# A store moved to POOL's DMA queue, and two steps of a DMA transpose shifted by a sub-step, in a macaron S4D block

## The chip, the cores and the metric

The kernel runs on one core of a Trainium2 chip. The time is that of the device, in microseconds (us), for one execution of the whole program. A core has five engines, each with its own in-order instruction stream: TensorE (PE; its weight loads are listed as PEld), VectorE (DVE), ScalarE (ACT), GpSimd (POOL) and SyncE (SP). SP only starts DMA transfers here; ACT and POOL start some as well. An instruction that waits holds up all that stands behind it in its stream.

## The reference

The input x has 8 sequences of 2048 tokens with 256 features. The block is

```python
x = x + 0.5 * ffn(layernorm(x))          # 256 -> 1024 -> relu -> 256
n = layernorm(x)
y = irfft(rfft(n) * rfft(K))[:length]    # causal convolution along the tokens, K from the S4D parameters
x = x + layernorm_affine(n + y + n * D)
x = x + 0.5 * ffn(layernorm(x))          # the same weights
```

with `K[h, l] = 2 Re sum_n Ct[h, n] exp(dtA[h, n] l)`: for each of the 256 features 64 complex exponentials.

## The kernel before

**Three stages.** Sublayer "a" is the first feed-forward part together with the normalization that follows it (0 to about 800 us). The convolution comes next (800 to 1000 us), and sublayer "b", the second feed-forward part, last. In "a" and "b" the tokens go through in 64 groups of 2 x 128. For each group PE makes 8 hidden chunks of 128 units: `up` (L854) needs 6 matmuls of 128x128 by 128x256, `down` (L864) another 6, since each factor is split into a high and a low part. ACT evicts the high part of a hidden chunk (`hx`, L926), DVE the low part (L116 with `hx`), and `down` follows three chunks later. Around each group there is other work: a bias addition on POOL (L777), statistics on DVE (L693, L697), small reciprocal and `q_u`, `nb_u` operations, normalizations on ACT (L730), transposes on PE (L794), a cast on ACT (L803), the closing addition `post_a` on DVE (L992). From group 44 on the transpose is made by DMA: `xp` is stored (L819) and read back turned (L823).

**The background.** While "a" runs, `matrices()` builds the tables of the convolution. It is a generator: `sublayer` draws steps from it between the hidden chunks. Its last part makes the matrix P in 32 blocks (bt 0 to 31) of 128 x 1024 numbers, and for each block both P itself (`o_dram`, used for the outputs) and its transpose (`pt_dram`, used for the states) must come to DRAM. A block passes four generators:

- `make(bt)`: six POOL operations (L600 to L610) write the block to one of four places in the big tile u (`p_of`, reused by block bt + 4).
- `spread(bt)`: ACT splits the block's 32-bit numbers into two planes of 16 bits (L620, two copies), SP stores the planes (`pv`, L623) and then the block itself (`o`, L625).
- `turn(bt)`: SP reads the planes back with a DMA transpose (L631).
- `transpose(bt)`: the join. DVE and ACT put the turned planes together in the block's place (L646, one copy each), and SP stores that (`pt`, L650).

The loop runs in cycles of six sub-steps. In cycle c the generators `transpose(c-3)`, `turn(c-2)`, `spread(c-1)` and `make(c)` each take one step a sub-step. `PX` is the number of sub-steps that `turn` lets pass first, `PY` the number that the join lets pass, `DI` the same for the copies. Beside it `lags()` runs, which adds POOL operations (L536 to L542) and small POOL DMAs (L570, four in a row) in the first 13 cycles or so.

**What sets the order.** Each engine's order is settled when the program is built. A scheduler places each operation by its own estimate of when its inputs are ready; operations marked `keep_in_program_order` stay in the order of the source among themselves. The turns, ACT's copies, the joins and L777 are so marked. The POOL operations of `make` aren't, so the scheduler may mix those of several blocks. A change in one place can thus reorder all the engines.

Of the kernel before, what the change touches and what calls it, by code (L numbers as in the profile page):

```python
# [43 lines left out]
def macaron_s4d_kernel(  # L44
# [17 lines left out]
    nc = tc.nc  # L62
# [152 lines left out]
    o_dram = [dram.tile([P, BCH * P], F32, name=f"o_{i}") for i in range(NBT)]  # L215
# [42 lines left out]
    def matrices():  # L258
# [207 lines left out]
        for i in range(H // P):  # L466
            nc.gpsimd.dma_start(
                out=kpad[i * P : (i + 1) * P, P + 1 :], in_=zeros[:, 0 : P - 1]
# [6 lines left out]
        with nc.allow_non_contiguous_dma(reason="256 numbers"):  # L475
            nc.gpsimd.dma_start(
                out=kpad.rearrange("(g c) k -> c g k", c=2)[:, :, P], in_=k0
# [100 lines left out]
        def p_of(bt):  # L578

            r, i = (room[2], 28 + bt % 4 * 8) if bt < first else (room[3], (16, 24, 48, 56)[bt % 4])  # L580
            return r[:, i * P : (i + 8) * P]

        def tmp_of(bt):
            tm = room[2][:, 60 * P : 64 * P] if bt < first else room[3][:, 0 : 4 * P]
            return tm.rearrange("p (g a b) -> p g a b", g=PB, a=NA)

        def make(bt):

            E = G_
            pp = p_of(bt).rearrange("p (r g k) -> p r g k", r=2, g=PB)  # L590
            tm = tmp_of(bt)
            gs = slice(bt * PB, (bt + 1) * PB)
            br, bi = (
                pb[:, ri, gs, ::-1].unsqueeze(2).to_broadcast([P, PB, NA, NB]) for ri in range(2)
            )
            ar, ai = (
                pa[:, ri, gs, ::-1].unsqueeze(3).to_broadcast([P, PB, NA, NB]) for ri in range(2)
            )
            pr, pi = (pp[:, ri].rearrange("p g (a b) -> p g a b", b=NB) for ri in range(2))
            E.tensor_mul(pr, br, ar)  # L600
            yield
            E.tensor_mul(tm, bi, ai)
            yield
            E.tensor_sub(pr, pr, tm)
            yield
            E.tensor_mul(pi, br, ai)
            yield
            E.tensor_mul(tm, bi, ar)
            yield
            E.tensor_add(pi, pi, tm)  # L610
            yield

        def spread(bt):

            pl = planes[:, bt % 2]
            pu = p_of(bt).bitcast(U16).rearrange("p (m w) -> p w m", w=2)
            for _ in range(DI):
                yield
            for w in range(2):
                tc.keep_in_program_order(A_.copy(pl[:, w], pu[:, w]))  # L620
                yield
            via = pv_dram[bt % 2]
            nc.sync.dma_start(out=via, in_=pl.rearrange("p w m -> p (w m)"))  # L623
            yield
            nc.sync.dma_start(out=o_dram[bt], in_=p_of(bt))  # L625
            yield

        def turn(bt):
            for _ in range(PX):
                yield  # L630
            ins = nc.sync.dma_start(  # L631
                out=planes[:, bt % 2].rearrange("p w (k n) -> p (w k) n", n=P),
                in_=pv_dram[bt % 2], transpose=True,
            )
            if PINT:
                tc.keep_in_program_order(ins)
            yield

        def transpose(bt):
            pl, ptb = planes[:, bt % 2], p_of(bt)  # L640
            for _ in range(PY):
                yield
# [9 lines left out]

        planes = wpool.tile([P, 2, 2, BCH * P], U16, name="planes", tag="wE")
        P_REINT = (V.tensor_copy, A_.copy)
        PY = 0
        BACK = 3
        DI = 2
        PX = 2
        PA = 9.1
        PB_ = 10.3  # L660
        PPIN = 1
# [2 lines left out]
        for bt in range(NBT + BACK):  # L664
            parts = []
            if 0 <= bt - BACK < NBT:
                parts.append(transpose(bt - BACK))
            if 0 <= bt - 2 < NBT:
                parts.append(turn(bt - 2))
            if 0 <= bt - 1 < NBT:  # L670
                parts.append(spread(bt - 1))
            if bt < NBT:
                parts.append(make(bt))
            for n in range(6):
                for p in parts:
                    next(p, None)
                next(beside, None)
                yield (PA if bt < first + BACK else PB_) / 6
            if bt == first + BACK - 1:
                yield "half"  # L680
# [554 lines left out]
    def begin():  # L1235
        for _ in range(sizes[1] // PB):
            next(head)

    sublayer(
        w1t, w2t, pre_a, post_a, 18, "a", load_weights(), chain(matrices(), early()),  # L1240
        {"half": NG // 2, "tables": NG * 3 // 4},
        {NG * SLOTS - 6: lambda: next(head), NG * SLOTS - 1: begin},
# [127 lines left out]
```

## Time and profile before

| what | value |
|---|---|
| median of 8 runs | 1762.92 us (1759.86 to 1769.06) |
| the profiled execution's own time | 1765.73 us |
| its span, first to last instruction | 1763.7 us |
| mean granted clock of TensorE | 0.994 |
| PE busy | 1726.4 us, 98% |
| DVE, ACT, POOL busy | 1369.7, 985.3, 589.4 us |
| blocks of P are made from / to | 194 us (first L600) / 598.6 us (last store pt) |
| `o`, `pv`, `pt` stores | 32 each, 512 KB, 3.6 us from issue to landing (median) |
| turn of planes | 32, 6.2 us from issue to landing (median) |
| L620 / L646 on ACT / L646 on DVE, median | 1.05 / 1.36 / 0.84 us |
| six operations of `make`, one each | 1.06 us (multiplications), 1.30 us (addition, subtraction) |

The 40 slices of the page show PE at 9 tenths or more in nearly all, and POOL full between about 180 and 330 us:

```profile
PE   8999999989999999999999799999999999999998
POOL 1117989875775115110000122222222222222220
```

In such a row each digit stands for 44 us. Timeline lines begin with start and length in us; a bracket at the end gives the idle time of the engine just before, and what ended it. "SPq" and "ACTq" are instructions that start a DMA; their length is that of the issue, not of the transfer.

### The profile page before, as it was taken

What the parts mean: (1) busy time and instruction counts of PE and PEld (TensorE: products, weight loads), DVE (VectorE), ACT (ScalarE), POOL (GpSimd) and SP (SyncE); (2) the same over time, 40 slices, a digit from 0 to 9 for tenths busy, and PEclk for the clock granted to TensorE, in tenths of its full rate; (3) what the DMA queues carried; (4) which work ended last, traced back from release to release, by engine and by line L of the source; (5) the groups of instructions that cost most, each with busy time, mean ns of one, the idle gap of its engine ahead of it and who ended that gap; (6) DMA issues with size and microseconds to landing.
All of it is one profiled execution on the core that took longest, in us unless ns stands there. A gap on an engine that the chain in (4) does not pass through costs nothing.

```text
span 1763.7 us, 40994 instructions
## 1 busy us (share of the span) xinstructions
PE 1726.4 (98%) x15367; PEld 1697.8 (96%) x15367; DVE 1369.7 (78%) x4405; ACT 985.3 (56%) x2178; POOL 589.4 (33%) x550
## 2 busy tenths in 40 slices
PE   8999999989999999999999799999999999999998
PEld 7999999989999999999999799999999999999998
DVE  6998877767776667766999788888888888888884
ACT  4555477667777755544555445555554555555553
POOL 1117989875775115110000122222222222222220
PEclk9999999999999999999999999999999999999999
DMA  5111177669878533346998813333333333333331
GB/s 189 49 37 52 49 216 225 212 190 269 233 230 240 162 103 96 93 113 193 263 268 261 267 52 93 97 91 86 95 91 97 91 96 94 87 94 94 92 94 50
DMA packets 293277, 242.68 MB, mean 138 GB/s; under 512 B 164564, under 2 KB 237012, under 8 KB 292566
## 3 DMA queue, kind: packets, MB, share of 16 engines
q1 hardware_dynamic: 265648, 206.36, 41.5%
q10 hardware_dynamic: 26502, 32.52, 5.6%
q8 instruction: 120, 1.97, 0.5%
q0 software_dynamic: 928, 1.19, 0.3%
q14 instruction: 79, 0.65, 0.1%
HBM read 91.89 MB, written 109.84 MB: 114 GB/s over the span
## 4 chain that ended last, share of the span: by engine, by line
PE 71%; DMA 5%; DVE 1%; SPq 1%; ACT 1%; POOL 0%; issue 0%; ACTq 0%; DVEq 0%; POOLq 0%
PE po_b L864 20%; PE ph_b L854 20%; PE ph_a L854 10%; PE po_a L864 10%; PE pv L1097 3%; PE py L1163 3%; PE py L1172 3%; DMA planes<-pv 2%; DMA pt<-pt 1%; DMA pt_b<-xp 0%; SPq L631 0%; DMA wb<-w_dram 0%; DMA ot<-o 0%; PE pe L1215 0%; DVE u L646 0%
## 5 line engine op out<-in xcount | busy, mean ns | idle before, releaser
L864 PE MATMUL po_a<-wa,hx_a 128*128 128x256 f32 x3072 | 456.1, 285 | 11.5 <-DVE hx_a L116 11.3
L854 PE MATMUL ph_a<-xh_a,wa 128*128 128x256 f32 x2048 | 456.2, 287 | 1.8 <-DVE wa L195 1.1
L864 PE MATMUL po_b<-wb,hx_b 128*128 128x256 f32 x3072 | 442.0, 283 | 2.7 <-DVE hx_b L116 2.6
L854 PE MATMUL ph_b<-xh_b,wb 128*128 128x256 f32 x2048 | 443.6, 284 | 0.7 <-ACT xh_b L803 0.7
L864 PEld LDWEIGHTS po_a<-wa,hx_a 128*128 128x128 f32 x3072 | 406.6, 192 | 14.3 <-DVE hx_a L116 13.8
L864 PEld LDWEIGHTS po_b<-wb,hx_b 128*128 128x128 f32 x3072 | 401.0, 192 | 3.4 <-DVE hx_b L116 3.3
L854 PEld LDWEIGHTS ph_a<-xh_a,wa 128*128 128x128 f32 x2048 | 355.9, 193 | 4.6 <-ACT wa L194 1.5
L854 PEld LDWEIGHTS ph_b<-xh_b,wb 128*128 128x128 f32 x2048 | 353.8, 193 | 1.1 <-ACT xh_b L803 1.1
L926 ACT ACTIVATE hx_b<-ph_b 128x256 fp32r<-128x256 f32 x512 | 191.4, 381 | 237.8 <-PE ph_b L854 226.0
L926 ACT ACTIVATE hx_a<-ph_a 128x256 fp32r<-128x256 f32 x512 | 194.7, 387 | 231.3 <-PE ph_a L854 220.8
L116 DVE SCALAR_TENSOR_TENSOR hx_a<-ph_a,hx_a 128x256 fp32r<-128x256 f32 x512 | 209.1, 414 | 123.3 <-ACT hx_a L926 121.7
L854 PE MATMUL ph_a<-xl_a,wa 128*128 128x256 f32 x1024 | 290.3, 285 | 0.0
L854 PE MATMUL ph_b<-xl_b,wb 128*128 128x256 f32 x1024 | 285.7, 284 | 0.0
L1305 POOL TENSOR_TENSOR xb<-xb,lnb_sb 128x512 f32<-128x512 f32 x64 | 83.1, 1300 | 510.3 <-DMA xb<-x_dram 341.7
L116 DVE SCALAR_TENSOR_TENSOR hx_b<-ph_b,hx_b 128x256 fp32r<-128x256 f32 x512 | 210.8, 414 | 52.6 <-ACT hx_b L926 45.4
L854 PEld LDWEIGHTS ph_a<-xl_a,wa 128*128 128x128 f32 x1024 | 197.5, 193 | 0.8 <-DVE xl_a L805 0.4
L854 PEld LDWEIGHTS ph_b<-xl_b,wb 128*128 128x128 f32 x1024 | 198.0, 193 | 0.1
L777 POOL TENSOR_TENSOR xa<-xa,hb 128x512 f32<-128x512 f32 x64 | 88.9, 1389 | 278.8 <-ACT xn L730 242.3
L730 ACT ACTIVATE xn<-xb,nb_fb,t_fb 128x255 f32<-128x255 f32 x127 | 69.5, 594 | 77.5 <-DVE nb_fb L116 77.5
L777 POOL TENSOR_TENSOR xb<-xb,hb 128x512 f32<-128x512 f32 x64 | 95.1, 1486 | 52.0 <-ACT xn L730 22.7
L815 DVE COPY pl_b<-xn 128x512 uint16<-128x512 uint16 x62 | 43.6, 703 | 72.9 <-ACT xn L730 72.9
L730 ACT ACTIVATE u<-xa,nb_u,t_u 128x256 f32<-128x256 f32 x104 | 90.2, 867 | 0.0
(263 smaller groups left out, 2510.4 us busy)
## 6 DMA issues: line engine op xcount, KB each, us to landing
o<-u SPq DMA_DIRECT2D x32, 512.0 KB, 3.6
pv<-planes SPq DMA_DIRECT2D x32, 512.0 KB, 3.6
pt<-u SPq DMA_DIRECT2D x32, 512.0 KB, 3.6
tz<-kpad SPq DMA_DIRECT2D x64, 256.0 KB, 4.7
xb<-x_dram SPq DMA_DIRECT2D x64, 256.0 KB, 2.7
out_dram<-xb SPq DMA_DIRECT2D x64, 256.0 KB, 2.9
x_dram<-xa ACTq DMA_DIRECT2D x62, 256.0 KB, 2.0
xp<-pl_b SPq DMA_DIRECT2D x62, 256.0 KB, 2.0
```

The source lines that it names most:

```text
L116: return V.scalar_tensor_tensor(out=o, in0=a, scalar=s, in1=b, op0=op0, op1=op1)
L730: ins = A_.activation(dst, src, AF.Identity, bias=nb[:, i : i + 1], scale=rs[:, i : i + 1])
L777: return G_.tensor_add(xt, xt, hb2.unsqueeze(1).to_broadcast([P, NTB, H]))
L815: copy(pl[:, w], xu[:, :, :, :, w])
L854: nc.tensor.matmul(ph, wt[wp][:, dc, fs], xp[:, dc, :], start=(n == 0), stop=(n == 3 * NDC - 1))
L864: nc.tensor.matmul(po[:, i, :], hp[:, tsl], wt[wp][:, fc, :], start=(fc == 0 and i == 0 and n == 0), stop=(fc == NFC - 1 and n == 2), skip ...
L926: last[A_] = A_.activation(hh, ph, AF.Relu)
L1097: ins = nc.tensor.matmul(pv[ri][c * N : (c + 1) * N, l, j0 * B : j1 * B], pts[c][:, l, ri * N : (ri + 1) * N], some(j0, j1)[:, :, BCH * bt ...
L1163: nc.tensor.matmul(py[c][:, l, :], ucs[c][:, l, :], tzs[c][:, l, :], start=(l == 0), stop=False, skip_group_check=True,)
L1172: nc.tensor.matmul(py[c][:, l, :], xs[cs, ri, p0 + l, :], ots[ri][cs, l, :], start=False, stop=(l == PB - 1 and ri == 1), skip_group_check ...
L1305: G_.tensor_add(xt, xt, lnb_sb.unsqueeze(1).to_broadcast([P, NTB, H]))
```

## The change

The store of the block leaves `spread` and SP's queue. It is issued in `make` by POOL (`nc.gpsimd.dma_start`), behind the block's sixth operation and before the step ends, so it waits for that operation alone. `spread` has one sub-step less. The turn lets one sub-step pass instead of two, the join lets one pass instead of none. What is computed stays the same.

```diff
@@ make(bt)
             E.tensor_add(pi, pi, tm)
+            nc.gpsimd.dma_start(out=o_dram[bt], in_=p_of(bt))
             yield
@@ spread(bt)
             via = pv_dram[bt % 2]
             nc.sync.dma_start(out=via, in_=pl.rearrange("p w m -> p (w m)"))
-            yield
-            nc.sync.dma_start(out=o_dram[bt], in_=p_of(bt))
             yield
@@ matrices()
-        PY = 0
+        PY = 1
         BACK = 3
         DI = 2
-        PX = 2
+        PX = 1
```

## The prediction

> **What bounds the kernel now.** I read, in this order, the page's busy shares, the table of busy time by stretch, the waits of each engine, the chain of waits, and single stretches of the timeline. TensorE (PE) is busy 98% of 1763.7 us, so a gain can only be where it stands still or runs slowly. The table by stretch (columns: stretch, length, then busy us and count of PE, PEld, DVE, ACT, POOL, then granted clock, DMA share, GB/s) says where:
>
> ```profile
> 300.00:340.00 40.00, 39.41 (x332) 39.20 (x331) 27.43 (x74) 24.46 (x49) 33.58 (x34) 1.00 0.61 183
> 340.00:380.00 40.00, 36.81 (x292) 36.41 (x293) 31.43 (x73) 26.75 (x54) 29.90 (x29) 0.96 0.66 211
> 380.00:420.00 40.00, 35.37 (x287) 34.26 (x286) 24.93 (x72) 29.46 (x53) 29.87 (x25) 1.00 0.98 264
> ...
> 460.00:500.00 40.00, 40.00 (x338) 40.00 (x337) 28.61 (x81) 29.40 (x58) 28.04 (x24) 1.00 0.80 221
> ...
> 540.00:580.00 40.00, 37.54 (x306) 37.34 (x304) 23.93 (x77) 29.91 (x59) 17.64 (x15) 0.97 0.76 225
> 580.00:620.00 40.00, 40.00 (x330) 39.99 (x330) 27.30 (x90) 27.93 (x59) 5.45 (x5) 0.98 0.59 161
> ```
>
> Full rate is 338 matmuls in 40 us (460 to 500). Against it, (338 − count)/338 x 40 gives the us lost: 0.7, 5.4, 6.0, 0, 3.8 and 0.9 in these rows, and 0.6 and 0.7 in 220 to 260 (333) and 420 to 460 (332): 18.1 us in all while the blocks of P are made. This is the ceiling: 1765.7 − 18.1 = 1747.6. Who holds PE is in the waits between 200 and 580 us (engine, waiting line, what ended the wait: us, times, longest):
>
> ```profile
> PE po_a L864 <- DVE hx_a L116: 11.3, 8, 3.1
> SPq L625 <- POOL u L610: 90.5, 17, 37.4
> ACT u L646 <- DMA planes<-pv: 21.0, 9, 4.9
> ACT planes L620 <- POOL u L610: 3.8, 4, 1.2
> DVE u L646 <- DMA planes<-pv: 14.6, 7, 4.2
> POOL u L600 <- DMA pt<-u: 16.8, 6, 5.6
> ```
>
> PE waits only for the hidden halves hx, which ACT and DVE evict. These are held when they stand at the join (L646) of planes whose turn has not landed. Block 12 on the timeline:
>
> ```profile
> 375.39 1.05 ACT L620 COPY planes<-u 128x1024 uint16<-128x1024 uint16 x1 [0.82 <-POOL u L610]
> ...
> 377.41 0.34 SPq L623 DMA_DIRECT2D pv<-planes  x1
> ...
> 380.82 4.25 SPq L631 DMA_TRANSPOSE planes<-pv  x1
> ...
> 387.96 1.36 ACT L646 COPY u<-planes 128x1024 uint16<-128x1024 uint16 x1 [3.08 <-DMA planes<-pv]
> ```
>
> The first copy starts the moment POOL ends the block; 12.6 us later the join can start, and ACT stood idle for 3.08 of them. Such joins make the losses of 300–340, 380–420 and 420–460: **A = 7.4 us**. The 5.4 us of 340–380 (**B**) are another thing: two tiny DVE operations, 160 ns elsewhere, that read two SBUF operands while POOL runs without a pause:
>
> ```profile
> 348.46 3.08 DVE L116 SCALAR_TENSOR_TENSOR q_u<-mv_j,t_u 128x4 f32<-128x4 f32 x1
> ...
> 352.79 1.98 DVE L116 SCALAR_TENSOR_TENSOR nb_u<-mv_j,t_u 128x4 f32<-128x4 f32 x1
> ```
>
> The 3.8 + 0.9 us after 540 (**C = 4.7**) are in the chain of waits: a turn of planes holds SP's queue, and the store xp of token group 45, ready at 564.9 (its second copy ends), goes out at 567.01.
>
> ```profile
> 562.80 4.11 SPq L631
> 567.01 3.11 DMA xp<-pl_a
> ```
>
> **The change part by part.** *Stores of P leave SP.* 32 issues of 0.33 us and 90.5 us of waiting go from SP's queue. But most of that wait lay before SP had other work: the planes' store follows the second copy within 0.1 us in 24 of 32 blocks, and in the critical blocks whose landing is recorded (10, 11, 13, 14) the turn follows the landing of that store within 1.1 us. So on the path this part earns nothing in A. In C it helps: in the built order of the changed program turn 29 stands ahead of the join's store pt and no turn stands between that and xp of group 45; xp can go at 564.9, 2.1 us sooner, and the slow clock after the gap falls too. I take 4 of the 4.7; bounds 0 (SP is late for another reason) and 4.7.
>
> *The turn a sub-step sooner.* From block 20 on it goes about 2.3 us earlier (block 22: issued at 478.58 behind the store pt at 478.17, its planes written by about 476). Joins there have no idle before them: cover, so 0. Without that cover it would be worth these 2.3 us a block.
>
> *The join a sub-step later.* From block 20 on it stands 1 hidden chunk (12 matmuls, 1.44 us) later. The store pt is then as much later, and so is POOL's L600 of the block four further on, which waits for its landing (16.8 us, 6 times, above). From block 20 POOL ends 10 to 20 us ahead of ACT's copies, which hides it: 0. In blocks 4 to 15 it doesn't: there POOL starts a block 0.2 to 5 us after that landing, so 1.44 us comes on top of POOL's lag.
>
> *Stores on POOL.* The trace has no 512 KB store on POOL. Nearest rows, ns shortest/median/longest:
>
> ```profile
> L570 POOL DMA_DIRECT2D kpad<-u x16: 528/530/847, 241.8 to 348.4; - x16
> L476 POOL DMA_DIRECT2D kpad<-u x1: 1114/1114/1114, 139.0 to 139.0; - x1
> ```
>
> and 550 to 609 for the two 256 KB stores of x1 (L1006). Bounds 0.53 and 1.11; I take 0.6, by L1006, which also stores 128 long rows, plus 0.1 for the wait on L610 (the gap that POOL shows between dependent operations): 0.7 x 32 = 22 us of POOL. Behind the waiting store stand the next block's L602 and the bias addition L777, for which post_a's addition (L992) and so a PSUM bank of po waits. After block 16 POOL is idle a quarter of the time and hides it. But between 256 and 334 us POOL has hardly a pause (39.16 of 40 us in 260–300), and eight stores before block 8 ends make 8 x 0.7 = 5.6 us of lag that nothing covers (bounds 8 x 0.53 = 4.2 and 8 x 1.21 = 9.7). The join now waits for the landing of the store on POOL's queue as well (2.3 to 4.5 us in the rows of L1006 and L570); it comes 10 us later or more, which hides it.
>
> *What the lag does.* The instruction order is fixed when the program is built, and it was built with that lag. In the changed order ACT's copies of blocks 5 to 11 stand 4 to 12 hidden chunks later, the joins 4 to 8. At two places a whole token group of DVE and ACT work has been pushed into the next one's: after hidden chunks 208 and 232 (counted from the first) PE has all "down" products behind it, and next in its order are transposes of a group not yet normalized. In the order of before no such place exists. Price after 208: from its eviction on, two small DVE operations 0.3, two normalizations 1.1, one of u 0.87, two copies of planes 2.1, the cast xh 0.6: 5.0 us, in which PE has 10 matmuls, 1.2: idle 3.8. DVE has 7.1 us of work in the four chunks before it (four hx 1.65, an addition 0.68, six bn_stats 2.5, six bn_aggr 1.0, eight small ones 1.3) against 5.8: 1.3 more. And the clock: in 340–380 5.4 us were lost for 3.19 idle, in 540–580 3.8 for 2.46, so 1.3 to 2.2 more, say 1.7. Sum 6.8. After 232 the join of block 11 stands in DVE's chain, 5 chunks = 7.2 us after its copies; copies to join took 10.9 us for block 11 before (356.71 to 367.57). Less DVE's surplus of 1.3 it waits 2.5; then join 0.84, three small 0.5, normalizations 2.0, cast 0.6: 6.4, minus 1.2 of PE work: 5.2, plus 1.3 and 1.7: 8.2. Joins of blocks 5, 8 and 14 stand 3 to 6 chunks behind their copies; waits of 3.1 and 4.9 left gaps of 1.0 and 2.7 in PE before, so a wait less some 2: 1.8 + 1.0 + 1.2 = 4.0. POOL's first blocks (ACT's L620 starts 0.03 us behind L610 in 3, 4, 5): 1. Together 20.0, in place of A + B + 0.6 = 13.4: **+6.6**. Bounds: −13.4 (nothing of it happens) and +17 (lag by the 1.11 row adds 4.1, a hold like B comes once more at 5.4, and the two places cost half as much again, 7.5).
>
> **Sum:** +6.6 − 4 = +2.6 on the profiled execution's 1765.7 (span 1763.7 plus 2.0 around it): 1768.3. That execution lies 2.8 above the median of the 8 runs, 1762.9, which would give 1765.5. I take 1767.
>
> The Trainium skill, SBUF — State Buffer, section "SBUF: two separate sides", speaks against a store on POOL: its descriptors are written through the port pair that DVE's fast copies lock, and it names 620 ns alone, 3100 beside a copy. Here 16 issues of L570 took at most 847 ns, so the trace does not show it; by the page's figures, an estimate, eight stores would lag by 20 us more and the time would be near 1787. TensorE: Matmul & The Clock Gate, "What's actually happening", lets the clock halve after an idle window of about 3.4 us; here 2.46 us were enough at 575 and 2.72 at 395 were not.
>
> **Rivals.** *Faster: the joins stop waiting.* PE on the chip takes 1.44 us or more a chunk; if POOL keeps up, the pushed-together groups fill up in time, and A and C go: 1765.7 − 12.1 = 1753.6, or 1750.8 on the median. For it: POOL has 15 us idle in 220–340. Against: most of it is L600 waiting for pt, which comes later now. *No change:* what the two places cost equals what A, B and C give back, and SP's freedom is hidden, as blocks 8 to 14, whose turn is bound by the store pv and not by SP, suggest; also the case that the turn isn't sooner at all. Its time is the median, 1763. *Slower by the port:* each store starts POOL anew and a q_u or nb_u is held as at 348; it decides if three more such holds fall where ACT waits: 3 x 5.4 = 16, so 1783. For it: the holds at 243.71 (3.60) and 348.46 both follow POOL's DMA issues of L570. Against: the other two bursts of L570 held nothing over 1.3.
>
> **How the numbers follow.** Chances: forecast 0.48, faster 0.22, no change 0.22, port 0.08. A measurement of this kernel tells 0.2%, 3.5 us, from no change. Of the forecast's 0.48, 0.10 fall within that and 0.01 below; of the no-change case 0.16 within and 0.03 to each side; of the faster case 0.02 within. So faster 0.01 + 0.03 + 0.20 = 0.24, within 0.10 + 0.16 + 0.02 = 0.28, slower 0.37 + 0.03 + 0.08 = 0.48. The range must hold 8 in 10: low 1756, which leaves out the lower 0.12 of the faster case, high 1779, which holds the lag by the 1.11 row and one more hold (1767 + 9.5) and leaves out the port case's 0.08. The forecast alone: 1762 to 1776.
>
> **What would show it.** Right: POOL's stores near 0.6 us; two PE gaps of 3 to 6 us between 325 and 400, each after four pushed-up "down" products, clock below 1 behind them; no gap near 575; joins without idle from block 17. Wrong: no PE gap over 3 us before 420 (faster), DVE's two-operand operations over 2 us at several stores (port), or POOL issues over 1 us (lag).

## The result, and the profile after

| | before | after |
|---|---|---|
| median | 1764.63 us (38 runs, 1759.86 to 1770.51) | 1772.58 us (13 runs, 1769.29 to 1778.76) |
| profiled execution, its span | 1765.73, 1763.7 us | 1771.62, 1769.9 us |
| granted clock of TensorE | 0.994 | 0.992 |

The ratio is 1.0045, 95% interval [1.0034, 1.0055]: slower by some 8 us. 1767 was forecast, with 1756 to 1779 as range. The sign and the stretch were right. The size was not: +2.6 was worked out for the profiled execution, and it rose by 5.9.

In the profile after, the store is L611, and lines from 626 on stand one lower than before (join L645, `up` L853, `down` L863). The table by stretch of the changed kernel (columns as before: length, busy us and count of PE, PEld, DVE, ACT, POOL, clock, DMA share, GB/s):

```profile
300.00:340.00 40.00, 38.48 (x320) 37.79 (x318) 26.92 (x69) 23.46 (x46) 37.44 (x39) 1.00 0.58 183
340.00:380.00 40.00, 37.23 (x290) 36.45 (x291) 24.45 (x66) 25.71 (x49) 27.73 (x28) 0.96 0.74 205
380.00:420.00 40.00, 32.35 (x238) 30.86 (x236) 27.55 (x59) 27.78 (x47) 33.64 (x32) 0.87 0.73 229
420.00:460.00 40.00, 38.70 (x312) 38.70 (x313) 25.94 (x76) 33.99 (x61) 22.96 (x22) 0.96 0.89 273
...
540.00:580.00 40.00, 40.00 (x334) 39.84 (x334) 30.34 (x84) 32.61 (x64) 27.01 (x24) 1.00 0.69 229
580.00:620.00 40.00, 39.60 (x323) 38.79 (x322) 28.58 (x92) 28.98 (x60) 4.59 (x4) 1.00 0.60 185
```

Against 338 matmuls, 26.4 us are lost between 220 and 620 us (18.1 before). The loss at 380 to 420 doubled, from 6.0 to 11.8; that of 540 to 580 went from 3.8 to 0.5. The waits between 200 and 580 us (engine, waiting line, what ended the wait: us, times, longest):

```profile
POOL u L600 <- DMA pt<-u: 34.6, 11, 9.0
ACT u L645 <- DMA planes<-pv: 11.9, 8, 4.4
DVE u L645 <- DMA planes<-pv: 8.1, 9, 2.1
POOL o L611 <- POOL u L610: 6.2, 21, 0.3
PE pt_a L793 <- ACT xn L729: 5.4, 2, 5.2
PE po_a L863 <- DVE hx_a L116: 5.3, 5, 2.4
```

The joins wait less for their planes than before (20.0 instead of 35.6), but PE now waits once for 5.2 us at a transpose, whose input ACT normalizes (L729), and POOL waits twice as long for the landing of `pt`. The store itself, by the view of its line (ns shortest/median/longest), and the time to landing:

```profile
L611 POOL DMA_DIRECT2D o<-u x32: 554/594/858, 220.4 to 571.7; - x32
...
DMA to landing us min/median/max: 3.0/4.0/6.9
```

0.59 us, and 21 of 32 times 0.3 us of waiting for L610 before it: 0.9 us in these blocks, 0.8 on the mean. The two largest gaps on the timeline of the changed kernel (start, length; in brackets the idle time before and what ended it):

```profile
333.75 2.26 DVE L116 SCALAR_TENSOR_TENSOR q_u<-q_u,s_u 128x4 f32<-128x4 f32 x2
...
341.14 0.74 PE L853 MATMUL ph_a<-xh_a,wa 128*128 128x256 f32 x4 [2.44 <-ACT xh_a L802]
...
379.19 2.99 DVE L116 SCALAR_TENSOR_TENSOR q_u<-mv_j,t_u 128x4 f32<-128x4 f32 x2
...
383.48 1.35 ACT L645 COPY u<-planes 128x1024 uint16<-128x1024 uint16 x1 [4.42 <-DMA planes<-pv]
385.53 1.09 ACT L729 ACTIVATE xn<-xa,nb_u,t_u 128x255 f32<-128x255 f32 x2 [0.69 <-DVE nb_u L116]
...
386.18 1.39 PE L793 MATMUL pt_a<-ident,xn 128*128 128x128 f32 x4 [5.21 <-ACT xn L729]
```

These are the two places after hidden chunks 208 and 232. At the first, q_u on DVE took 2.26 us for two operations and the normalization had to wait. At the second two things end together: q_u is held for 2.99, and ACT stands 4.42 us at a join whose planes are late.

Behind both gaps the granted clock is low for some microseconds (third number from the end; columns as in the table by stretch):

```profile
341.00:346.00 5.00, 4.86 (x26) 4.67 (x27) 1.54 (x3) 4.02 (x9) 4.01 (x4) 0.66 0.88 284
386.00:394.00 8.00, 7.13 (x33) 6.44 (x33) 2.56 (x8) 7.16 (x14) 5.24 (x5) 0.52 0.48 180
394.00:400.00 6.00, 6.00 (x53) 6.00 (x51) 3.76 (x5) 4.20 (x7) 5.60 (x6) 1.00 0.81 188
```

From 386 to 394 a matmul takes 0.22 us, from 394 to 400 it takes 0.11.

### The profile page after: what moved, and what is told of

The parts are those of the page before. It is cut to its first block, busy times and chain, and to the rows that moved or that the text cites. A ratio compares the mean times of both kernels' runs of the same rounds, so it can differ in the third digit from the quotient of the medians.

```text
span 1769.9 us, 41000 instructions
## 1 busy us (share of the span) xinstructions
PE 1730.5 (98%) x15367; PEld 1699.2 (96%) x15367; DVE 1383.4 (78%) x4405; ACT 988.7 (56%) x2178; POOL 606.4 (34%) x582
## 4 chain that ended last, share of the span: by engine, by line
PE 78%; DMA 10%; DVE 6%; ACT 3%; issue 1%; SPq 0%; ACTq 0%; DVEq 0%
PE po_b L863 18%; PE ph_b L853 18%; PE ph_a L853 16%; PE po_a L863 16%; PE py L1171 3%; PE py L1162 3%; PE pv L1096 3%; DMA planes<-pv 2%; DMA pt_b<-xp 1%; DMA xa<-in_L_attn_x_dram 1%; DMA pv<-planes 1%; DMA pt<-pt 1%; PE pt_a L793 1%; DMA pt_a<-xp 1%; DVE hx_b L116 1%
## 5 line engine op out<-in xcount | busy, mean ns | idle before, releaser
L853 PE MATMUL ph_a<-xh_a,wa 128*128 128x256 f32 x2048 | 456.8, 288 | 4.8 <-ACT xh_a L802 3.8
L863 PE MATMUL po_a<-wa,hx_a 128*128 128x256 f32 x3072 | 453.9, 285 | 5.5 <-DVE hx_a L116 5.3
L853 PE MATMUL ph_b<-xh_b,wb 128*128 128x256 f32 x2048 | 442.6, 284 | 2.0 <-ACT xh_b L834 1.4
L863 PE MATMUL po_b<-wb,hx_b 128*128 128x256 f32 x3072 | 442.0, 283 | 0.4
L863 PEld LDWEIGHTS po_a<-wa,hx_a 128*128 128x128 f32 x3072 | 404.8, 192 | 8.1 <-DVE hx_a L116 7.3
L863 PEld LDWEIGHTS po_b<-wb,hx_b 128*128 128x128 f32 x3072 | 400.7, 192 | 1.3 <-DVE hx_b L116 1.3
L853 PEld LDWEIGHTS ph_a<-xh_a,wa 128*128 128x128 f32 x2048 | 357.2, 194 | 8.5 <-ACT xh_a L802 4.8
L853 PEld LDWEIGHTS ph_b<-xh_b,wb 128*128 128x128 f32 x2048 | 352.5, 193 | 2.8 <-ACT xh_b L834 1.8
L853 PE MATMUL ph_a<-xl_a,wa 128*128 128x256 f32 x1024 | 292.4, 287 | 0.3 <-DVE xl_a L836 0.2
L853 PE MATMUL ph_b<-xl_b,wb 128*128 128x256 f32 x1024 | 284.9, 284 | 0.0
L853 PEld LDWEIGHTS ph_a<-xl_a,wa 128*128 128x128 f32 x1024 | 199.0, 194 | 2.1 <-DVE xl_a L836 1.1
L853 PEld LDWEIGHTS ph_b<-xl_b,wb 128*128 128x128 f32 x1024 | 197.2, 193 | 0.1
L729 ACT ACTIVATE xn<-xb,nb_fb,t_fb 128x255 f32<-128x255 f32 x127 | 69.5, 594 | 78.9 <-DVE nb_fb L116 78.9
L776 POOL TENSOR_TENSOR xb<-xb,hb 128x512 f32<-128x512 f32 x64 | 94.8, 1481 | 44.2 <-ACT xn L729 21.5
L729 ACT ACTIVATE u<-xa,nb_u,t_u 128x256 f32<-128x256 f32 x104 | 89.9, 864 | 0.0
```

The source lines that it names most:

```text
L729: ins = A_.activation(dst, src, AF.Identity, bias=nb[:, i : i + 1], scale=rs[:, i : i + 1])
L776: return G_.tensor_add(xt, xt, hb2.unsqueeze(1).to_broadcast([P, NTB, H]))
L853: nc.tensor.matmul(ph, wt[wp][:, dc, fs], xp[:, dc, :], start=(n == 0), stop=(n == 3 * NDC - 1))
L863: nc.tensor.matmul(po[:, i, :], hp[:, tsl], wt[wp][:, fc, :], start=(fc == 0 and i == 0 and n == 0), stop=(fc == NFC - 1 and n == 2), skip ...
```

## The experiments

Two theories were held against each other. *Order theory*: the loss is made by the instruction order that the scheduler ("planner" in the expectations) writes down, at the pushed places. *POOL-time theory*: about 1 us more of POOL per block is what costs, whoever writes the order. Besides them stood the *port theory* (the store's descriptors hold VectorE) and the *shift theory* (the shifted sub-steps cost). Ratios are against the kernel before, with 95% intervals; a difference between two kernels is that of their ratios, times 1764 us. "Lost" is the time lost at PE in 220 to 620 us, by the count of matmuls as above.

### Stores alone, shift alone

`e1_store_only` is the change with PX and PY left at 2 and 0; `e2_shift_only` sets them to 1 and 1 and leaves the store on SP.

```diff
# e1_store_only, against before
@@ make(bt)
+            nc.gpsimd.dma_start(out=o_dram[bt], in_=p_of(bt))
@@ spread(bt)
-            yield
-            nc.sync.dma_start(out=o_dram[bt], in_=p_of(bt))
# e2_shift_only, against before
-        PY = 0
+        PY = 1
-        PX = 2
+        PX = 1
```

> The store of P on POOL alone; turn and join stay where they were before (PX = 2, PY = 0). Order theory: the building of the program saw POOL late because of the stores and put all `down` products ahead of the next group's transposes after hidden chunks 208 and 232, and this costs the time; the built order of this kernel has both places, so it expects two PE gaps of 2 to 6 us between 330 and 400 us and a time 6 to 12 us above before. Shift theory (the turn a sub-step sooner and the join a sub-step later cost the time): within 3 us of before. Port theory (descriptor writing on POOL and DVE hold each other): 6 to 12 us above, but with DVE operations over 2 us all over the blocks and no gap at the two places.

> The shift alone (PX = 1, PY = 1); the store of P stays on SP. Its built order has neither of the two places. Order theory: no gap over 3 us for that reason, a time from 6 us below before (joins of blocks 17 and later and the transposes by DMA gain) to 2 us above. Shift theory: 6 to 12 us above before. Port theory: like before, within 3 us.

Measured: e1 1783.3 us, 1.0106 [1.0091, 1.0121], 36.6 us lost. e2 1762.89, 0.9995 [0.9984, 1.0005], 15.7 lost. So the store alone costs more than twice what the change costs, and also more than the 6 to 12 us that the order and port theories gave it; the shift alone costs nothing. With the store there, the shift gives back 0.6%, some 11 us. The waits of e1 say how:

```profile
ACT u L645 <- DMA planes<-pv: 23.0, 12, 6.9
DVE u L645 <- DMA planes<-pv: 13.0, 10, 2.6
```

36.0 us of joins that wait for planes, against 20.0 with the shift. The shift theory fell here.

### Which blocks

```diff
# e3_late_blocks, against after (e8_early_blocks: the two conditions exchanged)
@@ make(bt)
-            nc.gpsimd.dma_start(out=o_dram[bt], in_=p_of(bt))
+            if bt >= first:
+                nc.gpsimd.dma_start(out=o_dram[bt], in_=p_of(bt))
@@ spread(bt)
+            if bt < first:
+                nc.sync.dma_start(out=o_dram[bt], in_=p_of(bt))
+                yield
```

> As after, but the blocks 0 to 15 store P from SP as before, and only blocks 16 to 31 from POOL. POOL issues 16 stores of 0.6 us, and the built order has neither of the two places. Order theory: the loss of after is gone, time from 5 us below before to 2 us above. Port theory or POOL-time theory (each store costs its 0.9 us somewhere): half of after's loss stays, 3 to 6 us above before.

> The counterpart of e3_late_blocks: blocks 0 to 15 store from POOL, blocks 16 to 31 from SP, the rest as in the change. The places 208 and 232 are in its built order. Order theory and the theory that POOL's lag in the early blocks is what counts: like the changed kernel, 1771 us, 1767 to 1775. A cost per store: half of the 8 us, 1767 us, and e3_late_blocks would have shown the other half, which it did not.

Measured: e3 1764.12, 1.0003 [0.9992, 1.0014], 15.7 lost, as much as e2; e8 1783.05, 1.0093 [1.0075, 1.0111], 38.3 lost. Blocks 16 to 31 may store from POOL for nothing; all of the cost comes from blocks 0 to 15. That e8 is slower than the change itself, with half its stores on POOL, no theory had expected.

### The pace

```diff
# e4_pace, against before; e5_pace_after: the same line, against after
-        PA = 9.1
+        PA = 10.3
```

> The kernel before with one number changed: the background is drawn at 10.3 instead of 9.1 per cycle in the first 19 cycles, so that fewer POOL operations fall into each hidden chunk. In its built order the join stands 13 hidden chunks behind the copies for nearly all blocks, where before had 5 to 12 in blocks 5 to 15. Order theory: the joins find their planes landed, the 7.4 us lost to them go and some of the hold by POOL too: 5 to 12 us below before, unless the later end of the blocks meets the transposes by DMA of group 44 and on (+0 to 4). POOL-time theory: the same POOL work, spread out, no more than 3 us below.

> The changed kernel with one number more: the blocks are paced at PA = 10.3 instead of 9.1, as in e4_pace. All 32 stores stay on POOL, right behind the last operation. In the built order the two places after hidden chunks 208 and 232 at which a whole group's work was pushed into the next are gone. Order theory (the loss is made by the order that the planner writes down): the cost of the store goes with the places, 1753 us, 1750 to 1758, no gap of TensorE over 2 us between 330 and 400. POOL-time theory and port theory (each store costs POOL 0.9 us, or holds VectorE, whatever the order): some 6 us or more above e4_pace, 1759 to 1764.

Measured: e4 1752.91, 0.9944 [0.9930, 0.9959], only 6.5 lost; it beats both kernels. e5 1766.12, 1.0005 [0.9992, 1.0019], 21.5 lost. In e4's waits the joins hardly appear:

```profile
ACT u L646 <- DMA planes<-pv: 1.1, 1, 1.1
```

So the part A of the loss before is cured by making the blocks at a slower pace; nothing had to leave SP for that. That was the order theory's outcome; the POOL-time theory allowed a gain of 3 us at most. e5 has no pushed place, as the order theory asked, and yet stands 11 us above e4 (e5 has the shift as well, which e4 has not); that is the POOL-time theory's outcome, and more than its figure of 6.

### One more operation in place of the store

```diff
# e6_dummy_op, against e2_shift_only
             E.tensor_add(pi, pi, tm)
+            E.tensor_mul(tm[:, 0:4], bi[:, 0:4], ar[:, 0:4])
             yield
```

> The turn a sub-step sooner and the join a sub-step later as in the change, the store on SP as before, and in place of the store on POOL one more small multiplication of POOL, 4 columns wide, behind each block's last addition; its result is not used. No DMA is on POOL's queue for o, and POOL is busy with it far less than with a store. The planner, however, writes down the same pushed places as for the changed kernel (208, 232, 248). Order theory: 1770 us, 1766 to 1776, with gaps of TensorE near 338 and 381. POOL-time and port theory (what costs is the time or the descriptors of the stores): like e2_shift_only, 1763 us, 1760 to 1765.

Measured: 1785.23, 1.0110 [1.0097, 1.0123], 39.4 lost. The added multiplication does not change what is computed. It was larger than the expectation says: the first dimension of tm is that of the groups, and the view of the line shows all 512 columns.

```profile
L611 POOL TENSOR_TENSOR u<-u x32: 1049/1061/1506, 220.1 to 582.6; 128x512 f32<-128x512 f32 x32
```

It is thus no test of order against POOL's time: it has the pushed places and also 1.06 us of POOL per block, a little more than the store's 0.9. But it has no store of `o` on POOL, and costs 20 us more than e2. So a loss of this size needs no store on POOL's queue; the port theory, by which e6 would be like e2, fell as the one cause.

### POOL's operations pinned

```diff
# e7_pinned, against after: each of the six operations of make(bt)
+            k_ = tc.keep_in_program_order
-            E.tensor_mul(pr, br, ar)
+            k_(E.tensor_mul(pr, br, ar))
...
```

> The changed kernel with the six operations of each block's product kept in the order of the program, so that the planner mixes them differently with other work; all 32 stores on POOL, PA stays 9.1. The built order has no place at which fewer than two hidden chunks are pending, beyond the two at the start. Order theory: the time of e2_shift_only, 1763 us, 1758 to 1767, no gap over 2 us at 338 and 381. POOL-time and port theory: like the changed kernel, 1770 to 1775.

Measured: 1768.35, 1.0018 [1.0006, 1.0031], 21.4 lost, with gaps of PE of 2.5, 3.3 and 3.4 us at 325, 356 and 371. It lies between the two forecasts: half of the loss goes when the order changes, half stays without any pushed place. Each of the three gaps follows a DVE operation that took far longer than elsewhere while POOL was busy (a hold, in what follows): q_u, a join's copy (0.75 us elsewhere), and q_u again.

```profile
320.30 6.45 DVE L116 SCALAR_TENSOR_TENSOR q_u<-mv_j,t_u 128x4 f32<-128x4 f32 x1
...
352.31 6.42 DVE L646 COPY u<-planes 128x1024 uint16<-128x1024 uint16 x1
...
367.31 6.83 DVE L116 SCALAR_TENSOR_TENSOR q_u<-mv_j,t_u 128x4 f32<-128x4 f32 x1
```

The second started while POOL issued a DMA of L570, the third while it issued a store.

### The order held

DVE's and ACT's order in sublayer "a" is taken as the source draws it, so that copies and joins stand at the same hidden chunks in both kernels, and only where `o` is stored from differs. It was held from hidden chunk 110 to 420; the expectation gives half of these numbers.

```diff
# e9_held_sp, against e2_shift_only; e10_held_pool, against after
# e11_held_pool_pace is e10, e12_held_sp_pace is e9, with PA = 10.3
@@ sublayer
             if t == 0:
                 ordered.close()
+            if tag == "a" and t == 110:
+                ordered.enter_context(tc.manual_schedule(engines={mybir.EngineType.Activation, mybir.EngineType.DVE}))
+            if tag == "a" and t == 420:
+                ordered.close()
```

> The shift of the change with the store on SP (as e2_shift_only), and the order of VectorE and ScalarE in sublayer a, from hidden chunk 55 to 210, held as the source draws it, so that the planner's estimate of POOL no longer decides it. The copies of blocks 0 to 31 stand 7 hidden chunks apart and the joins 12 to 15 behind their copies. This is the base of the pair with e10_held_pool: near e2_shift_only, 1764 us, 1756 to 1772 by either theory.

> The changed kernel, stores on POOL, with the order of VectorE and ScalarE held in the same way: copies and joins stand at the same hidden chunks as in e9_held_sp, and no place is pushed. Only POOL's own time and order, and where o is issued, differ. Order theory (the planner's pushes alone cost): within 3 us of e9_held_sp. POOL-time theory (0.9 us a store, 8 stores before block 8 ends, make ScalarE's copies wait for POOL, whoever writes the order): 7 us or more above e9_held_sp, with waits of the copies (L621) on POOL's last operation (L610) between 250 and 400 us.

> As e10_held_pool, with the blocks paced at 10.3 instead of 9.1, which gives POOL some 1.3 us more a block, more than a store's 0.9. POOL-time theory: the gap to e12_held_sp_pace is smaller than that of the pair before, 0 to 4 us. Order theory: no gap in either pair.

> As e9_held_sp, paced at 10.3. By either theory the best of the four, near e4_pace: 1753 us, 1748 to 1758.

| | store from SP | store from POOL |
|---|---|---|
| PA 9.1 | e9 1779.22, 1.0075 [1.0054, 1.0096], 24.4 lost | e10 1796.96, 1.0175 [1.0151, 1.0200], 41.8 lost |
| PA 10.3 | e12 1774.25, 1.0047 [1.0029, 1.0065], 19.8 lost | e11 1794.59, 1.0168 [1.0144, 1.0193], 33.7 lost |

The held order is a bad one in itself (e9 is 14 us above e2, e12 18 above e4, where both were expected to be near them). But within each pair DVE and ACT have one order (in the traces the same instructions one by one until after 1030 us), and the store on POOL costs 18 and 21 us. The order theory, by which the pairs would agree, fell. That the pace would give POOL the time back fell too. The tables of e9 and e10 by stretch, 260 to 420:

```profile
260.00:300.00 40.00, 38.62 (x322) 38.21 (x322) 30.24 (x77) 28.73 (x55) 34.01 (x35) 1.00 0.69 220
300.00:340.00 40.00, 30.50 (x251) 29.69 (x249) 24.41 (x62) 21.81 (x41) 38.00 (x38) 0.97 0.57 184
340.00:380.00 40.00, 39.96 (x316) 39.73 (x317) 30.06 (x76) 28.92 (x56) 35.62 (x33) 0.94 0.74 233
380.00:420.00 40.00, 39.40 (x329) 39.19 (x329) 30.07 (x81) 29.49 (x57) 26.96 (x23) 1.00 0.81 270
```

and e10:

```profile
260.00:300.00 40.00, 35.35 (x283) 34.80 (x281) 27.77 (x71) 24.86 (x46) 36.75 (x39) 0.96 0.72 199
300.00:340.00 40.00, 34.45 (x257) 34.25 (x258) 30.52 (x64) 24.52 (x47) 35.38 (x38) 0.87 0.63 195
340.00:380.00 40.00, 32.59 (x252) 31.95 (x252) 26.92 (x60) 22.58 (x44) 33.34 (x33) 0.91 0.54 176
380.00:420.00 40.00, 35.01 (x278) 34.81 (x277) 29.61 (x67) 26.09 (x48) 29.23 (x29) 0.91 0.74 211
```

With the store from SP most of the loss is over at 340; with it on POOL it goes on to 420, and the clock falls with each gap. How far POOL lags shows in the end of the block's last operation (L610 on the timeline, us):

| block | e2 | after | later | e9 | e10 | later |
|---|---|---|---|---|---|---|
| 4 | 262.2 | 271.4 | 9.2 | 265.9 | 269.4 | 3.4 |
| 8 | 324.2 | 333.7 | 9.5 | 320.6 | 325.4 | 4.8 |
| 11 | 350.8 | 371.1 | 20.3 | 348.4 | 358.8 | 10.4 |
| 14 | 387.0 | 403.1 | 16.1 | 383.0 | 401.1 | 18.2 |

In the held pair 0.9 us a block would make 4.5, 8.1, 10.8 and 13.5 us; up to block 11 the measured lag is of this size or below, and then the time that PE itself lost comes on top.

The gaps of PE in e10 have two kinds of cause. Ahead of those at 261 (3.9 us), 299 (1.8) and 343 (5.6) ACT had stood 5.27, 4.80 and 6.44 us at the first copy of a block that POOL had not ended (L621, released by L610). But those at 317 (4.4), 369 (1.4) and 395 (5.0) follow a small operation of DVE that was held for 7.71, 5.55 and 7.04 us. The last on the timeline of e10, DVE, then POOL, then ACT:

```profile
392.74 7.04 DVE L116 SCALAR_TENSOR_TENSOR nb_u<-mv_j,t_u 128x4 f32<-128x4 f32 x1
...
392.57 0.62 POOL L611 DMA_DIRECT2D o<-u  x1 [0.30 <-POOL u L610]
393.21 1.07 POOL L602 TENSOR_TENSOR u<-u 128x512 f32<-128x512 f32 x1
...
398.71 1.05 POOL L608 TENSOR_TENSOR u<-u 128x512 f32<-128x512 f32 x1
399.83 1.28 POOL L610 TENSOR_TENSOR u<-u 128x512 f32<-128x512 f32 x1
...
399.81 1.09 ACT L729 ACTIVATE xn<-xa,nb_u,t_u 128x255 f32<-128x255 f32 x2 [4.96 <-DVE nb_u L116]
```

nb_u starts while POOL issues the store, is held through the six operations that follow without a pause, and ends at 399.78, 0.02 us after L608, where POOL pauses 0.08 us ahead of the dependent L610. In e9 only one q_u or nb_u took over 1.8 us (3.31 at 250.63). But ACT stands at copies for POOL in e9 as well, 14.1 us in all between 200 and 580 us (e10: 16.5). The two longest of these waits in e9, then those of e10:

```profile
320.60 1.04 ACT L620 COPY planes<-u 128x1024 uint16<-128x1024 uint16 x1 [5.99 <-POOL u L610]
...
338.07 1.04 ACT L620 COPY planes<-u 128x1024 uint16<-128x1024 uint16 x1 [5.98 <-POOL u L610]
```

```profile
262.84 1.04 ACT L621 COPY planes<-u 128x1024 uint16<-128x1024 uint16 x1 [5.27 <-POOL u L610]
...
346.71 1.04 ACT L621 COPY planes<-u 128x1024 uint16<-128x1024 uint16 x1 [6.44 <-POOL u L610]
```

So these waits, the sign that the expectation of e10 named, do not tell the two kernels apart. Of PE's gaps of 0.9 us or more between 220 and 420 us, e10 has 11.3 us behind copies that waited and 10.8 behind held operations of DVE; e9 has 8.1 and 1.3. In the pair at 10.3, e12 has no such gap there, and e11 has 5.3 us behind a copy and 6.0 behind a join's copy held for 5.30 us and a q_u held for 5.99. Of the idle time that the store adds to PE in this stretch, held operations thus bring 9.5 of 9.7 us in the one pair and 6.0 of 11.8 in the other, in the one profiled execution of each kernel.

## Why the prediction was right in sign and off in size

**Ceiling.** 18.1 us lost, 1747.6 at best: e4, which loses 6.5, has a profiled execution of 1751.49. This reading of the profile held.

**Stores of P leave SP, A: 0.** Not shown by itself, since with the store on POOL comes the lag. e4 shows that A can be had with the stores on SP.

**C: −4 of 4.7.** The gap near 575 is gone, as said. The rows from 540 to 620 lose 2.3 us instead of 4.7, so it brought 2.4. That SP's freedom did it isn't shown: e4 loses 4.5 there with the stores on SP and e1 3.3 with them on POOL.

**The turn a sub-step sooner, 0; the join later, 0.** Right by itself (e2: no change). But the cover named for it, joins without idle, is gone in the blocks that the store delays: there the pair is worth the 11 us between e1 and after. The forecast saw this case only for blocks 20 and on, and for the early blocks only the cost of the later join. That 1767 came so near is in part luck: it left out the 11 us that the shift gives back, and put the store too low by more than that.

**The store's price, 0.7.** The issue was sized right (0.6, measured 0.594). The wait ahead of it was taken as 0.1 and is 0.3 in 21 of the 32 blocks: 0.9 there.

**The lag, 5.6 us before block 8 ends.** 9.5 against e2, inside the bounds of 4.2 to 9.7, and 20.3 at block 11. This is a term that was sized too small, since delays feed back: POOL waits for `pt` four blocks on (34.6 us, 16.8 before).

**The two places, 6.8 + 8.2, and joins 4.0.** The places and their order were right: gaps at 338 and 381. The rows 300 to 380 lost 7.8, 380 to 460 14.9, together 22.7 against 19.0 for these terms. PE stood idle for 13.2 us of that, less than the 15.6 that the terms give without the clock; the other 9.5 were lost while it was busy, against 3.4 for the two clock terms of 1.7. So the term that was mis-sized is the clock behind the gaps: 0.66 from 341 to 346 and 0.52 from 386 to 394, 0.87 over the row 380 to 420. "Two small DVE operations 0.3" was too small as well: at the first place two q_u took 2.26, at the second four took 2.99 and 1.31, while POOL was busy. Other parts of these sums were too long, for the gaps came to 2.44 us instead of 3.8, and to 5.21 and 0.68 instead of 5.2. A third place, after chunk 248 with one product pending instead of none, was not named, but it shows no gap of its own: that of 2.4 at 419 follows the join of block 14, for whose planes DVE waited 2.14 us, and joins were priced. (Of the bounds given for all this, −13.4 counts from the kernel before, but +17 from the forecast's +6.6.) In all 24.1 us were lost outside of C's rows; 20.0 were forecast and 13.4 stood before, so +10.7 in place of +6.6. With C that makes +8.3 by count against +6.2 of span. Matmul by matmul, the changed kernel's trace is 7.6 us late where that of before stands at 620 us, 8.3 at 1000, 4.8 at 1100 and 6.2 at the end: most of the difference of 2 us arises behind the stretch with the blocks. Its cause stays open.

**The reason given, that the built order makes the loss.** In the changed kernel the two largest gaps do stand at the pushed places. But the places aren't needed for a loss, by the held pairs: with no pushed place the store costs 18 to 21 us. The cost depends on the order around the store: 19 us (before to e1), 9 (e2 to after), 4 (e2 to e7), 11 (e4 to e5, the shift in it). Why the scheduler's orders differ so, why e8 with half the stores costs more than all, and what of the 18 us in the held pair is due to POOL's own order, which was not held, stays open.

**Slower by the port, 0.08.** Three holds where ACT waits, 16 us and 1783, were named. Its mechanism is there: in the traces of all the kernels, between 200 and 600 us, of the q_u and nb_u that start while POOL issues a DMA 21 of 73 took over 1.8 us (mean 1.39), while POOL runs an operation 15 of 789 (mean 0.79), while POOL is idle none of 434 (mean 0.16). The hold of 2.2 us at the first place starts in a store (333.62 to 334.23). But in the changed kernel no hold reaches 3 us, and e6 loses as much as e1 and e8 with only the 16 issues of L570 on POOL and a longest hold of 3.60, as before. In the changed kernel the holds are thus a part of the price. In e7 all three gaps follow holds, and in the held pairs more than half of the added idle time comes by them; there each long hold spans several operations of POOL, and those at 311.81 and 363.73 in e10 began in an operation and not in an issue. How large a part is due to the issues alone was not measured. The Trainium skill, SBUF — State Buffer, section "Who interferes with whom", has the loser of the shared port pair blocked until the other's instruction ends; in e10 nb_u was held through the store and six operations, so the measurement differs. The issues of 3100 ns that the prediction weighed did not come here: 858 ns at most.

**What would show it.** Of the signs named, stores near 0.6, gaps between 325 and 400 behind pushed-up products, the clock below 1 behind them, and no gap near 575 came true; the first gap, at 2.44 us, was below the 3 to 6 named, and some joins beyond block 17 had idle before them again (block 18 1.28 us).

## What to carry to other kernels

An engine that is busy a third of the span can still stand in a closed ring of buffers (make, copy, store, turn, join, store, make again) that has no slack for a stretch; a transfer moved to it is paid in that stretch with its issue and its wait, here up to 0.9 us a block, and several times over where the ring feeds back or where a busier engine holds up another. Look for the slack block by block, and put the store on that engine only where it has some (blocks 16 to 31 here). Before work is moved between queues, try the pace at which the background is drawn: one number brought 10 us here, where the change cost 8.

## What the runs showed of the hardware

A small DVE operation that reads two operands from SBUF can be held not for one instruction of POOL but for a whole run of them. Of 36 holds of q_u or nb_u over 1.8 us in the traces between 200 and 600 us (0.16 us while POOL is idle), 32 ended 21 to 32 ns after the end of a POOL instruction; of the twelve over 3.5 us, ten ended where POOL then paused for at least 75 ns, because the next instruction depended on the last or waited, and the longest (7.71) had lain through seven ends of POOL instructions without a pause behind them. A hold was likeliest where the operation started while POOL issued a DMA (21 of 73, above). Where POOL's order mixes blocks so that no operation depends on the one ahead of it, as in e10 from 393 to 400, there was no such pause. A join's copy on DVE, which reads one operand, was held too, by up to 6.42 us instead of 0.75 (e7). A pause placed on purpose was not tried.
